# Normed tiles of the second pass turned through memory and VectorE instead of TensorE, with loads moved to GpSimd's queue

## The chip, the cores and the metric

The kernel runs on one core of a Trainium2 chip. The metric is device time in microseconds: the median of the runs shown, each the time of one execution. TensorE is written PE, VectorE DVE, ScalarE ACT, GpSimd POOL, and SP is the engine that here only issues DMAs.

## What is computed

Two layers on `x` of 8 x 32 x 32 x 512, all in float32:

```python
# layer 0: group norm, 8 heads of 64 over 1024 tokens, out projection, residual
xn  = group_norm(x) * gn_scale + gn_bias
q, k, v = split(xn @ w_qkv + b_qkv)
x   = x + (softmax(q @ k.T / 8 per head) @ v) @ w_out + b_out          # "mid"

# layer 1: attention on 256 sampled tokens, then a norm and an MLP
h   = layernorm(x) * ln_g + ln_b                                       # "hat"
o   = gelu(depthwise_conv7x7(h @ wq + bq, stride 2) + dw_b)
pos = grid + tanh(o @ pw_w)                                            # 256 places per image
s   = bilinear_sample(x, pos)                                          # "smp"
q   = (h @ wq + bq) @ mq_w + mq_b;  k = (s @ wv + bv) @ mk_w + mk_b;  v likewise
z   = softmax(q @ k.T per head) @ v @ mo_w + mo_b + x
out = gelu((layernorm(z) * ln_g + ln_b) @ mlp_w + mlp_b) + z
```

## The kernel before

The kernel makes two passes over the images. The first (layer 0) writes two things to memory: the residual `mid` and the normed, turned features `hat_d`. It also does most of the convolutions. The second pass, which the change concerns, goes over 16 half images `hi`, and over 4 head pairs `hp` in each: 64 units, numbered `n`. A unit computes scores for 512 queries of two heads, their softmax, its turn, and the product with the values.

The order of work inside a pass is written out by hand. `at(place, step)` puts a step at a place on a line whose whole numbers are units, and `run_due` issues all steps sorted by place. Each engine then executes its instructions in that order, each waiting for what it reads and for a free buffer. Inside a plain unit the steps are:

- `scores` at n: PE makes `sc`, DVE the negated maxima `nmax`, ACT the exponentials `e`.
- `moved` at n + 0.02 and n + 0.04, `taken` at n + 0.0401 and n + 0.041: DVE turns 32x32 blocks of `e` into `sq`; SP writes `sq_d` and reads it back as `et`, so that the keys lie on the partitions. `share` and `spread` send the reciprocal sums the same way (`rs_d`, `inv`).
- `query_step` at n + 0.042: PE's product of `hat_h` and the folded weight `wA`, for the next unit's queries.
- `product` at n + 1.1 and `scale` at n + 1.2: PE's `av` of the unit before, and DVE's `attH`.

Beside them, `back_steps` finishes one tile of 128 tokens per unit, four tiles per half image:

- `fetch` and `add`: a residual tile `xr` from `mid`, to which POOL adds a bias row. They come in pairs of tiles.
- `joined`: PE multiplies `attH` with `wo`, DVE adds `xr` to give `z`, and takes its statistics (`stats`, `mv`); POOL raises the variance to the power -0.5.
- `norm`: DVE makes the normed tile `zn`.
- `turned`: PE transposes `zn` in four pieces of 128x128, and ACT copies the result as `zT` from PSUM.
- `mlp`, `biased`, `gelu`, `end`: the product of `zT` with `wm` (its rows scaled by `ln_g`), a bias row, gelu on ACT for two tiles at a time, then POOL adds `z` and stores the tile.

Three more strands are laid between. `conv_steps` makes the convolutions of the last two images, in chunks of 49 taps on two lanes: DVE alone (`chunk<-pad,dww,chunk`, five taps a unit, three in some), and ACT with POOL (`parts`, then `chunk<-parts,chunk`); each chunk begins with two products `mm<-wq_r,hat`. These taps run in about the first 36 units. `point_steps`, once per image, turns a finished convolution into places (`offsets`, `targets`), gathers the rows (`gather`) and weighs them on DVE (`sample`); `key_step` and `value_step` then multiply `smp`. `fetch_hat` loads a half image of `hat_d`, 1 MB, in one DMA.

The buffers that matter: three PSUM tiles `mm` that all of these products share, two buffers each for `et`, `zn`, `zT` and `hat_h`, and four for `xr`.

In the profile nearly all instructions carry line 54, since the helper `InOrder` records every operation there; they are told apart by their tiles. Matmuls in float32 appear as two records each.

Of the kernel before, what the change touches and what calls it, by code (L numbers as in the profile page):

```python
# [17 lines left out]
P = 128  # L18
# [3 lines left out]
C = 512  # L22
# [225 lines left out]
def attention_then_deformable_attention(  # L248
# [126 lines left out]
    def at(place, step):  # L375
        due.append((place, len(due), step))
# [654 lines left out]
    with ExitStack() as l1:  # L1031
# [15 lines left out]
        def load_small():  # L1047
            with nc.allow_non_contiguous_dma(reason="small vectors onto partitions"):
                for t, v in ((lng, ln_g), (lnb, ln_b)):
                    nc.sync.dma_start(t, v.rearrange("(c p) -> p c", p=P))  # L1050

        def load_conv():
            nc.sync.dma_start(dww, dw_w.rearrange("(c p) a u v -> p c (a u v)", p=P))
# [32 lines left out]
        def conv_load(b):  # L1086
            room[b, "o"] = cv.tile([P, NC, NS], F32, tag="o", name="o")
            nc.sync.dma_start(room[b, "o"], o_d[b][:, :, :])
# [27 lines left out]
        def offsets_turned(b):  # L1116
            room["th"] = turn_offsets(room["tanh"])
# [29 lines left out]
        def fetch_hat(hi):  # L1147
            hat[hi] = raw.tile([P, NC, C], F32, tag="hat", name="hat_h", bufs=2)
            nc.sync.dma_start(hat[hi], hat_d[hi // 2][:, ts(hi % 2, NC), :])

# [23 lines left out]
        def tmp(name, bufs):  # L1177
            return work.tile([P, C], F32, tag=name, name=name, bufs=bufs)

        def back_steps(hi, start, step, tail=False):  # L1180

            b, half = divmod(hi, 2)
            xs = mid[b].rearrange("(t p e) c -> e t p c", e=2, p=P)[half]
            outs = out_tok[b].rearrange("(t p e) c -> e t p c", e=2, p=P)[half]
            xr, z, zn, zT, res = {}, {}, {}, {}, {}
            n_units = 2 * B * NHP

            def fetch(t):
                xr[t] = tmp("xr", 4)
                nc.sync.dma_start(xr[t], xs[t])  # L1190

            def add(t):
                nc.gpsimd.tensor_tensor(xr[t], xr[t], bo_row, ALU.add)

            def joined(t):
                ps = project(lambda c: attH[hi][:, c, ts(t, P)], lambda c: wo[:, c, :])
                z[t] = tmp("z", 4)
                nc.vector.tensor_tensor(z[t], ps, xr[t], ALU.add)
                stats = work.tile([P, 6], F32, tag="stats", name="stats")
                mv = xr["mv", t] = work.tile([P, 3], F32, tag="mv", name="mv")  # L1200
                nc.vector.bn_stats(stats, z[t])
                nc.vector.bn_aggr(mv[:, 0:2], stats)
                rstd(mv[:, 2:3], mv[:, 1:2], 1e-5)

            def norm(t):
                zn[t], mv = tmp("zn", 2), xr["mv", t]
                nc.vector.tensor_scalar(
                    zn[t], z[t], mv[:, 0:1], mv[:, 2:3], ALU.subtract, ALU.mult
                )

            def turned(t):
                ps = mm_tile()
                for c in range(NC):
                    nc.tensor.transpose(ps[:, ts(c, P)], zn[t][:, ts(c, P)], ident)
                zT[t] = tmp("zT", 2)
                for half in range(2):
                    nc.scalar.copy(zT[t][:, ts(half, C // 2)], ps[:, ts(half, C // 2)])

            def mlp(t):
                res["ps", t] = project(lambda c: zT[t][:, ts(c, P)], lambda c: wm[:, c, :])  # L1220

            def biased(t):
                res[t] = tmp("res", 3)
                nc.vector.tensor_tensor(res[t], res["ps", t], bm_row, ALU.add)

            def gelu(t):
                nc.scalar.activation(res[t], res[t], AF.Gelu)

            def end(t):
                (nc.vector if tail else nc.gpsimd).tensor_tensor(res[t], res[t], z[t], ALU.add)  # L1230
                (nc.sync if tail else nc.gpsimd).dma_start(outs[t], res[t])

            for t in range(NC):
                over, eve = (start + step * t >= n_units - i and not tail for i in range(2))
                n, pair = start + step * t, start + step * (t - t % 2)

                ends = (n + 0.6, n + 1.03, n + 1.0392)
                if eve:
                    ends = (n + 0.61, n + 0.72, n + 0.73) if over else (n + 1.06, n + 1.62, n + 1.625)
                places = (pair - 1.6, pair - 0.5), (n + 0.012, n + 0.03), ends  # L1240
                if tail:
                    turn = n + 0.15 + 0.005 * (t > 0)
                    places = (n - 0.7, n - 0.6), (n, n + 0.01), (turn, n + 0.25, n + 0.26)
                steps = (fetch, add), (joined, norm), (turned, mlp, biased)
                for place, what in zip(sum(places, ()), sum(steps, ())):
                    at(place, lambda t=t, what=what: what(t))


                ends = [t - 1, t] if t % 2 and not tail else [t] if tail else []

                for what, after in (
                    (gelu, 0.27 if tail else 0.735 if over else 1.72),
                    (end, 0.28 if tail else 0.74 if over else 2.24),
                ):
                    for i in ends:
                        at(n + after, lambda i=i, what=what: what(i))
# [33 lines left out]
        def conv_steps():  # L1290
            for lane, chunks in enumerate(((0, 3, 6), (1, 2, 4, 5, 7))):
                free = 0.5 + lane
                for k in chunks:
                    b, cb = EARLY + k // NC, k % NC
                    first = next(n for n in range(60) if n + 0.49 > free)
                    fills = [first + 0.49, first + 0.55]
                    at(fills[0] - 1.8, lambda b=b, cb=cb: conv_fetch(b, cb))
                    for par, place in enumerate(fills):
                        at(place, lambda b=b, cb=cb, par=par: fill(b, cb, par))
                        at(place + 0.02, lambda lane=lane, par=par: fill_end(lane, par))  # L1300
                    unit = int(fills[1]) + 1
                    i = 0
                    while i < KS * KS:
                        points = unit % (2 * NHP) in (NHP - 1, NHP, NHP + 2)
                        count = 7 if lane else 3 if points else 5
                        for j in range(count):
                            if i == KS * KS:
                                break
                            place = 0.25 + 0.01 * j if not lane else 0.045 + 0.001 * j if j < 4 else 0.65 + 0.01 * j
                            at(unit + place, lambda b=b, cb=cb, i=i, lane=lane: tap(b, cb, i, lane))  # L1310
                            free = unit + place
                            i += 1
                        unit += 1

        def point_steps(b):
            last = 2 * NHP * b - NHP
            at(last - 3.5, lambda: conv_load(b))
            at(last - 2.035, lambda: conv_gelu(b))
            at(last - 1.465, lambda: offsets(b))
            at(last - 1.36, lambda: offsets_turned(b))  # L1320
            at(last - 0.959, lambda: targets(b))
            for h, (p0, p1) in enumerate(((-0.28, 0.0415), (1.72, 2.0415))):
                at(last + p0, lambda h=h: gather(b, h))
                at(last + p1, lambda h=h: sample(b, h))
            first = 2 * NHP * b
            for hp, place in enumerate((-0.82, -0.815, 0.185, 1.18)):
                at(first + place, lambda hp=hp: key_step(b, hp))
            for t, place in enumerate((-0.81, 0.18)):
                at(first + place, lambda t=t: value_step(b, t))

        def load_late():
            nonlocal bq_row, wo, wm, bo_row, bm_row, wq_r
            wo = load_w(late2, mo_w, "wo")
            wm = load_w(late2, mlp_w, "wm")
            bo_row = load_row(late, mo_b, "bo_row")
            bm_row = load_row(late2, mlp_b, "bm_row")
            bq_row = load_row(wp, bq, "bq_row")
            load_conv()
            wq_r = load_w(first, wq, "wq_r")
# [21 lines left out]
            point_steps(b)  # L1361
        for hi in range(2 * B):
            if hi > 1:
                at(NHP * (hi - 1) - 1, lambda hi=hi: fetch_hat(hi))
            if hi + 1 < 2 * B:
                back_steps(hi, NHP * (hi + 1) + 1, 1)
            else:
                back_steps(hi, NHP * (hi + 1) + 0.65, 0.1, tail=True)
# [34 lines left out]
```

## Time and profile before

| | |
|---|---|
| median of 3 runs | 3359.01 us (3353.66 to 3364.82) |
| profiled execution | 3361.59 us, of which the span 3359.9 us |
| mean granted TensorE clock | 0.991 |
| the second pass begins | about 2155 us into the span |
| busy time in the span | PE 3274.0, DVE 2496.4, ACT 1810.1, POOL 1545.1 us |
| moved by DMA | 643.61 MB, mean 192 GB/s |

All numbers in the steps below come from this one profiled execution. Busy time of PE is an upper view, because matmuls are pipelined and their ends are modelled. Where an engine waited for several things, the profile names the one that came last. Where a group's mean is larger than busy time divided by count, its instructions overlapped.

### The profile page before, as it was taken

Reading aid. Unit: us, or ns where it says so; the run is one execution under the profiler, and the core shown is the slowest. Engines: PE = TensorE matmul, PEld = TensorE weight load, DVE = VectorE, ACT = ScalarE, POOL = GpSimd, SP = SyncE. Lnnn points to the kernel's source line nnn. Section 1 sums busy time; section 2 is a strip of 40 time slices with the busy share of each in tenths; the row PEclk is TensorE's granted clock in tenths of the full one; section 3 lists DMA queues with packets and bytes.
Section 4 is the critical chain, followed back from the end, with each engine's and each line's share of the span. In section 5 each row is a group of like instructions: output and inputs, shape, how many; then the busy total and the mean of one; then the engine's idle time right before and its main releaser. Section 6 shows DMA issues by size and latency. Waiting matters only on the chain.

```text
span 3359.9 us, 59630 instructions
## 1 busy us (share of the span) xinstructions
PE 3274.0 (97%) x21736; PEld 1335.3 (40%) x21736; DVE 2496.4 (74%) x3381; ACT 1810.1 (54%) x3927; POOL 1545.1 (46%) x1905
## 2 busy tenths in 40 slices
PE   7999999999999999999999999889999999999998
PEld 3344444344444344344444443333333333333333
DVE  5777778888888898888888886348677686665654
ACT  3443356576576566566566564135566555654442
POOL 1001226746746755765665663205555454642222
PEclk9999999999999999999999999899999999999999
DMA  5666766776776767776766667356666565665753
GB/s 151 178 181 163 208 180 184 226 182 183 213 194 174 220 193 187 203 203 176 216 195 172 199 193 218 117 195 220 193 206 200 191 203 185 214 219 191 228 178 131
DMA packets 442180, 643.61 MB, mean 192 GB/s; under 512 B 73152, under 2 KB 236992, under 8 KB 439840
## 3 DMA queue, kind: packets, MB, share of 16 engines
q1 hardware_dynamic: 409232, 531.93, 55.0%
q0 software_dynamic: 30928, 104.73, 10.0%
q8 instruction: 172, 2.82, 0.3%
q10 hardware_dynamic: 1728, 3.15, 0.2%
q14 instruction: 120, 0.98, 0.1%
HBM read 247.43 MB, written 123.73 MB: 110 GB/s over the span
## 4 chain that ended last, share of the span: by engine, by line
PE 88%; DVE 3%; ACT 3%; POOL 2%; issue 2%; DMA 1%; SPq 0%; ACTq 0%; POOLq 0%; DVEq 0%
PE mm L54 55%; PE sc L54 17%; PE av L54 16%; ACT e L54 2%; POOL chunk L54 1%; DVE nmax L54 1%; DVE sq L54 1%; DMA et<-sq 1%; SPq L54 0%; POOL res L54 0%; POOL xr L54 0%; DMA row<-mid,ii 0%; DVE smp L54 0%; DVE stats L54 0%; ACT parts L54 0%
## 5 line engine op out<-in xcount | busy, mean ns | idle before, releaser
L54 ACT ACTIVATE e<-sc,nmax 128x1024 f32<-128x1024 f32 (+1 forms) x1024 | 803.1, 797 | 487.7 <-DVE nmax L54 486.3
L54 DVE TENSOR_REDUCE nmax<-sc 128x1 f32<-128x1024 f32 (+1 forms) x640 | 751.6, 1215 | 343.4 <-PE sc L54 343.0
L54 POOL TENSOR_TENSOR oa<-part_x,oa 128x256 f32<-128x256 f32 x852 | 638.6, 750 | 551.8 <-ACT part_x L54 505.6
L54 DVE STREAM_TRANSPOSE sq<-e 128x1024 f32<-128x1024 f32 x640 | 766.1, 1228 | 158.1 <-ACT e L54 137.8
L54 ACT ACTIVATE part_x<-pad_x,dww_x 128x256 f32<-128x256 f32 x852 | 441.6, 545 | 253.1 <-POOL oa L54 251.5
L54 PE MATMUL sc<-k,q 64*64 64x512 f32 x4096 | 516.2, 604 | 10.2 <-ACT e L54 7.2
L54 PE MATMUL av<-et,v 128*64 128x256 f32 x4096 | 501.2, 387 | 9.2 <-DMA et<-sq 5.5
L54 PEld LDWEIGHTS av<-et,v 128*64 128x64 f32 x4096 | 273.8, 137 | 325.9 <-issue 158.0
L54 POOL TENSOR_TENSOR mv<-mv,minus_half 128x1 f32<-128x1 f32 x128 | 76.5, 598 | 500.7 <-DVE mv L54 500.3
L54 POOL TENSOR_TENSOR chunk<-parts,chunk 128x256 f32<-128x256 f32 x240 | 188.2, 784 | 256.8 <-ACT parts L54 242.7
L54 PEld LDWEIGHTS sc<-k,q 64*64 64x64 f32 x4096 | 139.5, 132 | 317.7 <-issue 206.4
L54 PE MATMUL mm<-w,attT 128*64 128x512 f32 x1024 | 233.8, 600 | 11.7 <-DVE attT L54 11.7
L54 PE MATMUL mm<-xT,wB 128*64 128x512 f32 x1024 | 233.0, 597 | 3.2 <-issue 3.2
L54 DVE SCALAR_TENSOR_TENSOR od<-pad_x,dww_x,od 128x256 f32<-128x256 f32 x276 | 231.1, 837 | 5.5
L54 PE MATMUL mm<-wo,attH 128*64 128x512 f32 x1024 | 234.7, 600 | 0.0
L54 PE MATMUL mm<-wC,xT 128*64 128x256 f32 x2048 | 232.1, 379 | 0.0
L54 PE MATMUL mm<-wm,zT 128*64 128x512 f32 x1024 | 230.7, 592 | 1.0 <-ACT zT L54 1.0
L54 PE MATMUL mm<-hat_h,wA 128*64 128x512 f32 x1024 | 230.9, 593 | 0.0
L54 PE MATMUL mm<-xT,wA 128*64 128x512 f32 x1024 | 230.7, 592 | 0.0
L54 ACT ACTIVATION_READ_ACCUMULATOR e<-sc,nmax 128x1 f32 x1024 | 209.4, 204 | 0.0
L54 ACT ACTIVATE parts<-pad,dww 128x256 f32<-128x256 f32 x240 | 126.4, 552 | 126.9 <-POOL chunk L54 125.9
L54 PEld LDWEIGHTS mm<-wC,xT 128*64 128x64 f32 x2048 | 147.6, 137 | 78.1 <-issue 6.4
(182 smaller groups left out, 3503.7 us busy)
## 6 DMA issues: line engine op xcount, KB each, us to landing
et<-sq SPq DMA_DIRECT2D x2048, 128.0 KB, 2.9
sq_d<-sq SPq DMA_DIRECT2D x128, 512.0 KB, 2.7
et<-sq_d SPq DMA_DIRECT2D x128, 512.0 KB, 4.4
inv<-rs_d SPq DMA_DIRECT2D x256, 128.0 KB, 4.7
hat_h<-hat_d SPq DMA_DIRECT2D x16, 1024.0 KB, 8.3
xr<-mid SPq DMA_DIRECT2D x64, 256.0 KB, 5.7
xr<-in_x_dram POOLq DMA_DIRECT2D x62, 256.0 KB, 3.9
x<-in_x_dram POOLq DMA_DIRECT2D x60, 256.0 KB, 4.3
```

The costliest lines, as they stand in the source:

```text
L54: return self.tc.keep_in_program_order(op(*args, **kwargs))
```

## The change

In 58 of the 64 tiles of the second pass, PE no longer transposes `zn`. Instead the normed tile is written to memory (`away`), read back with its tokens and channels regrouped so that every 32x32 block already lies in the right place (`back`), and the blocks are turned by one DVE instruction (`blocks`), which gives `zT` directly. The four tiles of the tail and the last two before them keep the transposes (`by_matmul`). The channel order on the partitions differs between the two layouts, so the rows of `wm`, `ln_g` and `ln_b` are loaded in the new order, with four DMAs each, and the six remaining tiles write `zn` with its channels regrouped.

The residual rows are fetched by POOL's queue instead of SP's, and earlier (2.6 units ahead of the pair instead of 1.6; the add 1.45 instead of 0.5). From the third half image on, `hat_h` comes in four quarters by POOL's queue, one per unit.

Places change too: `mlp` follows the product for the next queries instead of preceding it, `biased` follows later in the unit, `end` comes at the beginning of a unit, the steps of `point_steps` come about a unit earlier, and the units with a sample have two DVE taps instead of three.

```diff
@@ load_small: the same for ln_g and ln_b
-                    nc.sync.dma_start(t, v.rearrange("(c p) -> p c", p=P))
+                    for r in range(NSQ):
+                        nc.sync.dma_start(
+                            t[ts(r, SQ)], v.rearrange("(r c i) -> r i c", r=NSQ, c=NC)[r]
+                        )
@@ beside fetch_hat, which still loads the first two half images
+        def fetch_part(hi, c):
+            if c == 0:
+                hat[hi] = raw.tile([P, NC, C], F32, tag="hat", name="hat_h", bufs=2)
+            nc.gpsimd.dma_start(hat[hi][:, c, :], hat_d[hi // 2][:, hi % 2 * NC + c, :])
@@ back_steps
             def fetch(t):
                 xr[t] = tmp("xr", 4)
-                nc.sync.dma_start(xr[t], xs[t])
+                nc.gpsimd.dma_start(xr[t], xs[t])
...
             def norm(t):
                 zn[t], mv = tmp("zn", 2), xr["mv", t]
+                to, src = zn[t], z[t]
+                if by_matmul(t):
+                    to = to.rearrange("p (c r i) -> p r c i", r=NSQ, c=NC)
+                    src = src.rearrange("p (r c i) -> p r c i", r=NSQ, c=NC)
                 nc.vector.tensor_scalar(
-                    zn[t], z[t], mv[:, 0:1], mv[:, 2:3], ALU.subtract, ALU.mult
+                    to, src, mv[:, 0:1], mv[:, 2:3], ALU.subtract, ALU.mult
+                )
+
+            def by_matmul(t):
+                return tail or start + step * t >= n_units - 1
+
+            def away(t):
+                zn["d", t] = dram.tile([NSQ, P, P], F32, tag="zn_d", name="zn_d", bufs=3)
+                nc.sync.dma_start(
+                    zn["d", t].rearrange("r p x -> p r x"), zn[t].rearrange("p (r x) -> p r x", r=NSQ)
+                )
+
+            def back(t):
+                zn["l", t] = tmp("zn", 2)
+                nc.sync.dma_start(
+                    zn["l", t], zn["d", t].rearrange("r (q k) x -> (r q) (k x)", k=NSQ)
+                )
+
+            def blocks(t):
+                zT[t] = tmp("zT", 2)
+                nc.vector.transpose(
+                    zT[t].rearrange("p (c q k) -> p k c q", c=NC, q=SQ),
+                    zn["l", t].rearrange("p (k c i) -> p k c i", k=NSQ, i=SQ),
                 )
...
-                ends = (n + 0.6, n + 1.03, n + 1.0392)
+                ends = (n + 0.0301, n + 0.0405, n + 1.013, n + 1.05, n + 1.15)
...
-                places = (pair - 1.6, pair - 0.5), (n + 0.012, n + 0.03), ends
+                places = (pair - 2.6, pair - 1.45), (n + 0.012, n + 0.03), ends
...
-                steps = (fetch, add), (joined, norm), (turned, mlp, biased)
+                turns = (turned,) if by_matmul(t) else (away, back, blocks)
+                steps = (fetch, add), (joined, norm), (*turns, mlp, biased)
...
-                    (end, 0.28 if tail else 0.74 if over else 2.24),
+                    (end, 0.28 if tail else 0.74 if over else 2.0125),
@@ conv_steps
-                        points = unit % (2 * NHP) in (NHP - 1, NHP, NHP + 2)
-                        count = 7 if lane else 3 if points else 5
+                        points = unit % (2 * NHP) in (NHP - 1, NHP + 1)
+                        count = 7 if lane else 2 if points else 5
@@ point_steps
-            at(last - 3.5, lambda: conv_load(b))
-            at(last - 2.035, lambda: conv_gelu(b))
-            at(last - 1.465, lambda: offsets(b))
-            at(last - 1.36, lambda: offsets_turned(b))
-            at(last - 0.959, lambda: targets(b))
-            for h, (p0, p1) in enumerate(((-0.28, 0.0415), (1.72, 2.0415))):
+            at(last - 4.5, lambda: conv_load(b))
+            at(last - 3.035, lambda: conv_gelu(b))
+            at(last - 2.465, lambda: offsets(b))
+            at(last - 2.36, lambda: offsets_turned(b))
+            at(last - 1.959, lambda: targets(b))
+            for h, (p0, p1) in enumerate(((-1.4, -0.959), (0.0125, 1.041))):
                 at(last + p0, lambda h=h: gather(b, h))
                 at(last + p1, lambda h=h: sample(b, h))
@@ load_late
-            wm = load_w(late2, mlp_w, "wm")
+            wm = late2.tile([P, NC, C], F32, tag="wm", name="wm")
+            for r in range(NSQ):
+                nc.sync.dma_start(
+                    wm[ts(r, SQ)], mlp_w.rearrange("(r c i) o -> r i c o", r=NSQ, c=NC)[r]
+                )
@@ the loop over half images
             if hi > 1:
-                at(NHP * (hi - 1) - 1, lambda hi=hi: fetch_hat(hi))
+                for c in range(NC):
+                    place = NHP * (hi - 1) - 1 + (c + 0.65 if c < NC - 1 else NC - 0.7)
+                    at(place, lambda hi=hi, c=c: fetch_part(hi, c))
```

## The prediction

> **What bounds the kernel now.** I read the page first, for the engines over the whole span.
>
> ```profile
> PE 3274.0 (97%) x21736; PEld 1335.3 (40%) x21736; DVE 2496.4 (74%) x3381; ACT 1810.1 (54%) x3927; POOL 1545.1 (46%) x1905
> ...
> PE   7999999999999999999999999889999999999998
> ```
>
> PE is busy in nearly every slice. Since a busy PE may still be slow, the second view is the table by stretches, for the second pass (columns: stretch, length, busy time of PE, PEld, DVE, ACT and POOL with instruction counts, granted clock, DMA share, GB/s). The first row lies in the part of the pass that also runs the convolution taps, the second behind it.
>
> ```profile
> 2400.00:2600.00 200.00, 198.67 (x1220) 74.77 (x1216) 146.80 (x255) 118.02 (x318) 109.68 (x129) 1.00 0.62 203
> 3000.00:3200.00 200.00, 200.00 (x1266) 77.28 (x1264) 124.94 (x194) 90.02 (x267) 57.59 (x62) 1.00 0.65 211
> ```
>
> The clock is full, and DVE, the next engine, has 27% left with the taps and 38% without. Third, PE in order of time for one plain unit (start, us, engine, operation).
>
> ```profile
> 3015.61 1.96 PE L54 MATMUL sc<-keys,q 64*64 64x256 f32 x32
> 3017.50 3.65 PE L54 MATMUL mm<-wo,attH 128*64 128x512 f32 x16
> 3020.98 3.60 PE L54 MATMUL mm<-wm,zT 128*64 128x512 f32 x16
> 3024.42 3.60 PE L54 MATMUL mm<-hat_h,wA 128*64 128x512 f32 x16
> 3027.85 1.89 PE L54 MATMUL av<-et,vals 128*64 128x512 f32 x8
> 3029.67 0.66 PE L54 MATMUL mm<-ident,zn 128*128 128x128 f32 x4
> 3030.25 1.96 PE L54 MATMUL sc<-keys,q 64*64 64x256 f32 x32
> ```
>
> There is no gap. A plain unit lasts 14.64 us, and from the start of the four transposes to the next scores 0.58 us pass: that is what a tile's transposes cost. The three units before it last 14.64 or 14.65 too, so PE's own work sets the pace. Last, whom PE waited for from 2160 us on.
>
> ```profile
> PE mm L54 <- DVE smp L54: 13.3, 2, 9.0
> PE mm L54 <- DVE zn L54: 5.1, 5, 1.3
> PE mm L54 <- DVE res L54: 4.7, 3, 1.6
> PE sc L54 <- ACT q L54: 4.4, 2, 4.0
> ```
>
> The 13.3 us are the two gathers that open the pass, which stay. What can be won beyond the transposes is about 10 us.
>
> **The change, part by part.** Rows for the costs, from the groups of 2150 to 3360 us and from the DMA issues (last number: us from issue to landing):
>
> ```profile
> L54 PE MATMUL mm<-ident,zn 128*128 128x128 f32 x256 | 41.9, 286 | 5.1 <-DVE zn L54 5.1
> L54 ACT COPY zT<-mm 128x256 f32<-128x256 f32 x128 | 41.1, 372 | 76.5 <-PE mm L54 75.1
> L54 DVE STREAM_TRANSPOSE sq<-e 128x1024 f32<-128x1024 f32 x128 | 158.5, 1238 | 54.2 <-ACT e L54 54.2
> L54 POOL DMA_DIRECT2D out_dram<-res x60 | 35.2, 587 | 21.9 <-POOL res L54 17.2 <-issue 4.6
> ```
>
> ```profile
> sq_d<-sq SPq DMA_DIRECT2D x128, 512.0 KB, 2.7
> et<-sq_d SPq DMA_DIRECT2D x128, 512.0 KB, 4.4
> ...
> xr<-mid SPq DMA_DIRECT2D x64, 256.0 KB, 5.7
> ```
>
> *Removed from PE.* Of 64 tiles, 4 in the tail and the 2 at n = 63 and 64 keep the transposes; 58 lose them: 58 x 0.58 = 33.6 us, all on PE's path. (Busy time gives 58 x 41.9/64 = 38.0; I take the spacing.) The 5.1 us in which PE waited for zn go too, as PE no longer reads it in these tiles. The Trainium skill ("VectorE: DVE Perf Modes", section on the three transpose paths) gives 390 ns for one 128x128 bf16 transpose on TensorE, which would make 58 x 4 x 0.39 = 90 us; no row here shows that price. It also says that VectorE turns blocks of 32x32 only, which is why a trip through memory has to move the blocks.
>
> *Removed from ACT.* 116 copies of 372 ns, 43 us. ACT waits for others here: 0 on the path.
>
> *Added to DVE.* 58 block transposes of 128x512. Half of the 128x1024 row (1238 ns) is 0.62 us; the writes go out four elements apart, which no row shows, so the upper end is 1.24 (half speed), the lower 0.5 (the spacing of the simplest 128x512 operation, zn). I take 0.62, since the taps that read at stride two show no loss for it (339 ns for 256 elements, against 615 for zn's 512). It stands between the statistics and the first sq transpose, where DVE waited 54.2 us in all for e. That cover hides it in units without lag; without cover it costs what is worked out below.
>
> *Added to SP's queue.* 58 writes and 58 reads of 256 KB. The write waits for zn; behind it wait rs_d and the second sq_d, both fed by later DVE work, so it delays nothing. The read waits for the write, and for its place behind the first et load, which itself waits for the end of av. Behind it stand the second et load and inv. So the read is issued at about 14.7 us of a plain unit, the write having landed long before (sq_d, twice as large: 2.7 us). Landing: 4.4 us (et) at best, 5.7 (xr of the same size, issued later in the same burst) taken. The new deadline: wm follows wo and wA now, so starts 1.89 + 3.49 + 3.43 = 8.8 us into the next unit of 14.06 us; less 0.6 for the block transpose, the data must be there 14.06 + 8.8 - 0.6 - 14.7 = 7.5 us after issue. It fits by 1.8 us. The second et load comes about 1 us later and is needed only at 26 us, where about 20 is expected: 0.
>
> *Moved to POOL's queue.* 64 residual rows and 56 quarters of hat: 120 x 0.587 = 70 us over 1140 us, on an engine that stood 344 us waiting for mv and 243 us for parts. They are issued one unit ahead or more and no longer stand in SP's burst: 0 on PE. The bound is an indirect issue (982 ns), 118 us in all, still inside these waits. DVE pays, if at all, through contention, and the trace has it (DVE in order of time):
>
> ```profile
> 2531.39 2.56 DVE L54 SCALAR_TENSOR_TENSOR chunk<-pad,dww,chunk 128x256 f32<-128x256 f32 x5
> ...
> 2605.98 5.55 DVE L54 SCALAR_TENSOR_TENSOR chunk<-pad,dww,chunk 128x256 f32<-128x256 f32 x3
> ```
>
> 0.51 us a tap while POOL stood still, 1.85 while it added xr and res. The adds stay, and mostly shift within the unit. An issue's cost to the taps: between 0 and its own length, 0.59 us; I take 0, since the issue writes no tile. The rule against the move is in the Trainium skill, "SBUF — State Buffer", section on the wrong bandwidth-pool intuition: a DMA from GpSimd's queue took 3100 ns instead of 620 when a DVE copy held the shared port. By that figure 120 issues would cost POOL 300 us more and the gain would shrink to the second rival's; the 587 ns above were measured beside a busy DVE and do not show it.
>
> *The new wait: wm for zT.* Without lag DVE runs: nmax ends 4.2 us after the scores began, z waits for wo until 5.4, z and statistics take 1.74 (2613.71 to 2615.45 in that unit), the block transpose 0.6, so zT stands at 7.8, before 8.8. If DVE is free only D us into a unit, zT comes at D + 2.3 + 1.7 + 0.7 = D + 4.7, and PE stalls D - 4.1. In a tap unit DVE ends with attH at 14.55 (av's end) and five taps (0.51 to 1.1 each, mean 0.77): 18.4, so D = 4.3, stall 0.2. With a sample (4.0 to 5.0) and two taps: about 19, D = 5, stall 0.9. This bites where PE has no extra product: 13 units of the tap part (11 to 13, 19 to 22, 27 to 30, 35, 36). 13 x 0.5 = 7 us taken; 0 to 20 as bounds, with slow taps and a slow block transpose. The same places lost time before, through zn and res.
>
> *The point steps a unit earlier, two taps instead of three.* The samples end a unit sooner than the keys need them: of the 4.7 us for res I take back 2 (0 to 4.7). The 4.0 us wait for q comes in the short units 3 to 5 that have no wm; a sample takes the place of the targets there: +1 (0 to +2).
>
> *Opening and tail.* Nine more DMA issues of some 0.4 us on SP, ahead of loads that PE needs 20 us later, while PE waits for gathers: 0 (to +3.6). Tail: four residual rows by POOL, where the add waited 4.7 us for them: 0 (-2 to +3).
>
> Sum: -33.6 - 5.1 - 2 + 7 + 1 = -32.7 us. The profiled execution took 3361.6 us (span 3359.9 and 1.7 around it), so 3328.9; it lay 2.6 us above the median of 3359.0, so **3326 us** as a median.
>
> **Rivals.** *DVE lag eats half* (0.2): taps near 1.1 us or a 1.24 us block transpose make each of the 13 units stall 2 us: 26 instead of 7, so 3326 + 19 = 3345. For it: 1.85 us taps occur, and the tolerance of PE falls, since zT now hangs on this unit's DVE. Against it: the xr adds, which made z wait 10.6 us, come a unit earlier.
>
> *The read lands late: slower* (0.1). One mechanism: the read sits between the two et loads on SP, and past 7.5 us from issue every plain unit stalls by the excess. There are 30 of them (the 13, units 37 and 38, and 15 later ones). It decides against the change past 7.5 + 32.7/30 = 8.6 us. At 9.5 us: 3326 + 60 = 3386. For it: the hat loads of the convolution, 512 KB in 512-byte pieces, take 8.6 us, and DMA share must rise from 0.65. The addition: 0.52 MB on 211 x 14.64 = 3.09 MB, so 257 GB/s. Against it: single microseconds behind the scores ran at 300 to 348 GB/s.
>
> *More than the sum* (0.1): the rest of the waits for res (2.7) and that for q (4.0 and the 1 added) vanish, and no new ones (7) come: 3326 - 14.7 = 3311.
>
> *It does not do what it says:* the written-out order has 58 writes, 58 reads, 120 moved loads and six tiles with transposes left, so only PE's "busy" could deceive; the gapless 14.64 us units speak against that.
>
> **How the numbers follow.** Forecast 0.6, lag 0.2, late read 0.1, more 0.1. The range, 3309 to 3348, reaches to the case of more and to the lag rival with a few us of scatter between runs, and leaves out the late read and the worst lag. Faster by over 0.3% (10 us, about what a measurement of this kernel can tell from no change): 0.6 + 0.1 + most of the lag case, 0.82; same 0.06; slower 0.12.
>
> **What would show it.** Right: plain units of 14.06 us in the table behind the taps, mm<-ident,zn at x24, PE's wait for DVE zT below 10 us, the read landing in 5 to 6 us, DVE busy up by 36 us. Wrong: waits of mm for zT above 30 us; if DVE then waits for the DMA zn<-zn_d it was the late read, if not the lag; or POOL issues far above 0.6 us.

## The result, and the profile after

| | before | after |
|---|---|---|
| median of the runs taken together | 3361.6 us | 3393.4 us (3379.4 to 3394.8) |
| ratio, 95% interval | | 1.0079 (1.0059 to 1.0099) |
| profiled execution, span | 3359.9 us | 3386.7 us |
| first scores of the second pass at | 2216.6 us | 2225.7 us |
| from there to the last unit's scores | 1078.2 us | 1094.2 us |

The kernel became slower by 32 us by the medians (27 by the ratio), where 33 us less had been forecast; the time lies outside the range. The last two rows use the start of the first `sc` matmul of a unit in the timeline of PE. They divide the 26.8 us of the spans into 3.1 in the first pass (the same instructions; it ends here with the last wait of `mm` for `attT`), 6.0 at the opening of the second, 16.0 in the units and 1.7 in the tail.

The page first (engines, and PE's slices), then the table by stretches for the two stretches that were shown of before, with the same columns.

```profile
PE 3254.8 (96%) x21504; PEld 1322.3 (39%) x21504; DVE 2546.2 (75%) x3439; ACT 1791.1 (53%) x3823; POOL 1607.8 (47%) x2025
...
PE   7999999999999999999999999789999989999998
```

```profile
2400.00:2600.00 200.00, 191.41 (x1174) 71.32 (x1174) 152.40 (x234) 107.80 (x288) 114.32 (x141) 0.99 0.73 231
3000.00:3200.00 200.00, 187.04 (x1162) 70.56 (x1162) 127.78 (x206) 83.38 (x242) 67.84 (x84) 0.99 0.79 244
```

The transposes are gone from 58 tiles (the group of those that are left, from 2150 us on):

```profile
L54 PE MATMUL mm<-ident,zn 128*128 128x128 f32 x24 | 3.9, 285 | 0.3 <-DVE zn L54 0.3
```

PE's busy time fell by 19 us only, of 38 in the transposes, partly since other matmuls became slower (last section). And PE, which was busy for all 200 us of the second stretch before, now stands still for 13 of them. No other engine is near its limit. So the loss is made of waits and of what follows them. PE in order of time shows where:

```profile
3128.28 1.96 PE L54 MATMUL sc<-keys,q 64*64 64x256 f32 x32
...
3140.49 3.65 PE L54 MATMUL mm<-wm,zT 128*64 128x512 f32 x16 [3.23 <-DVE zT L54]
...
3145.79 1.96 PE L54 MATMUL sc<-keys,q 64*64 64x256 f32 x32
...
3159.84 1.53 PE L54 MATMUL sc<-keys,q 64*64 64x256 f32 x24
```

The second of these two units lasts 14.05 us, 0.59 less than a plain unit before, as the sum had it. The first lasts 17.51: PE waits 3.23 us for `zT`. Behind the taps such a wait comes in six units (43, 45, 47, 51, 53 and 55). Over the second pass (whom PE waited for: us, times, longest):

```profile
PE mm L54 <- DVE zT L54: 42.3, 21, 3.8
PE mm L54 <- DVE smp L54: 17.8, 2, 11.1
PE av L54 <- DMA et<-sq_d: 5.3, 3, 3.2
PE mm L54 <- DMA hat_h<-hat_d: 3.5, 2, 3.2
```

Of the 42.3 us, 24.6 fall before 2920 us (taps) and 17.7 behind. Behind, but for one of 3.1 in the last unit, VectorE itself was waiting, for the read. The next lines follow the late one above. SP issued the read at 3128.84, when POOL had just issued two stores, a quarter of `hat_h` and two residual rows; four gathers followed from 3129.10 on. VectorE got the data at 3139.26.

```profile
3128.84 1.58 SPq L54 DMA_DIRECT2D zn<-zn_d  x1
```

```profile
3126.58 0.54 POOL L54 DMA_DIRECT2D hat_h<-hat_d  x1
3127.11 1.07 POOL L54 DMA_DIRECT2D xr<-mid  x2
```

```profile
3139.26 1.09 DVE L54 STREAM_TRANSPOSE zT<-zn 128x512 f32<-128x512 f32 x1 [3.49 <-DMA zn<-zn_d]
```

```profile
3128.00:3134.00 6.00, 6.00 (x52) 2.47 (x52) 4.39 (x14) 2.39 (x11) 4.08 (x5) 1.00 1.01 311
3134.00:3140.00 6.00, 3.26 (x16) 0.86 (x12) 2.41 (x5) 3.96 (x9) 3.59 (x4) 1.00 1.07 357
```

From issue to use 10.4 us passed, against a deadline of 7.5. In the two stretches of 6 us the DMA engines are full (share 1.01 and 1.07), although the mean over 3000 to 3200 is 0.79. Who had them: queue by queue (q0 is POOL's, q1 SP's; packets, MB, share of the engines' time) in the 6.76 us from the read's issue on, and in the same stretch of the same unit of a_sp, which has the rows and `hat_h` back on SP's queue:

```profile
q0 software_dynamic: 383, 1.24, 52.6%
q1 hardware_dynamic: 637, 0.97, 48.2%
```

```profile
q1 hardware_dynamic: 1172, 1.55, 73.6%
q0 software_dynamic: 178, 0.54, 21.1%
```

With the loads on it, POOL's queue had half of the engines, and SP's queue moved 0.97 MB where it moves 1.55. The median does not show this; the groups of DMA issues say 4.9 us for the read:

```profile
xr<-mid POOLq DMA_DIRECT2D x64, 256.0 KB, 6.3
zn<-zn_d SPq DMA_DIRECT2D x58, 256.0 KB, 4.9
```

### The profile page after: what moved, and what is told of

Its sections match the earlier page's. It is cut to its first block, busy times and chain, and to the rows that moved or that the text cites. A ratio compares the mean times of both kernels' runs of the same rounds, so it can differ in the third digit from the quotient of the medians.

```text
span 3386.7 us, 59407 instructions
## 1 busy us (share of the span) xinstructions
PE 3254.8 (96%) x21504; PEld 1322.3 (39%) x21504; DVE 2546.2 (75%) x3439; ACT 1791.1 (53%) x3823; POOL 1607.8 (47%) x2025
## 4 chain that ended last, share of the span: by engine, by line
PE 82%; DMA 5%; DVE 4%; POOL 4%; issue 2%; ACT 2%; SPq 1%; ACTq 0%; POOLq 0%; DVEq 0%
PE mm L54 51%; PE sc L54 16%; PE av L54 16%; DMA zn<-zn_d 2%; POOL chunk L54 1%; ACT e L54 1%; SPq L54 1%; DMA et<-sq 1%; DVE nmax L54 1%; DVE sq L54 1%; POOL xr L54 1%; DMA hat_h<-hat_d 1%; POOL row L54 1%; POOL res L54 0%; DMA zn_d<-zn 0%
## 5 line engine op out<-in xcount | busy, mean ns | idle before, releaser
L54 PE MATMUL mm<-wm,zT 128*64 128x512 f32 x1024 | 238.3, 608 | 43.4 <-DVE zT L54 42.3
```

Of the source, the lines that this page charges most:

```text
L54: return self.tc.keep_in_program_order(op(*args, **kwargs))
```

## The experiments

All comparisons are with runs of before on the same chip. "Units 0-43" and "43-63" are lengths in the profiled execution, from scores to scores: the part with taps (its last few units have none) and the part behind. Each is from one execution: h_small and after, whose units are the same, differ by 1.6 and 2.1 us, so a difference of about 2 us there shows nothing.

| kernel | ratio to before (95%) | units 0-43 | units 43-63 |
|---|---|---|---|
| before | 1 | 755.1 | 323.1 |
| after | 1.0079 (1.0059 to 1.0099) | 764.8 | 329.5 |
| a_sp: loads back to SP | 0.9984 (0.9973 to 0.9996) | 748.6 | 316.7 |
| a_xr: rows back | 1.0030 (1.0020 to 1.0040) | 761.5 | 319.4 |
| a_hat: quarters back | 1.0021 (1.0009 to 1.0032) | 752.8 | 322.4 |
| q_act: loads by ACT | 1.0036 (1.0021 to 1.0051) | 750.6 | 326.8 |
| b_pool: before, loads by POOL | 1.0079 (1.0064 to 1.0094) | 779.3 | 323.1 |
| a_busy: a_sp, POOL kept as busy | 0.9993 (0.9982 to 1.0004) | 750.8 | 316.4 |
| c_dense: after, dense transpose | 1.0085 (1.0071 to 1.0099) | 759.4 | 333.0 |
| a_dense: a_sp, dense transpose | 0.9971 (0.9960 to 0.9983) | 746.8 | 314.9 |
| a_fewtap: a_sp, 20 taps less | 0.9974 (0.9962 to 0.9986) | 740.8 | 317.9 |
| f_wm: after, wm behind av | 1.0114 (1.0096 to 1.0132) | 764.8 | 347.8 |
| d_split: before, split loads | 1.0022 (1.0013 to 1.0031) | 755.2 | 323.1 |
| h_small: after, loads later | 1.0074 (1.0053 to 1.0094) | 763.2 | 331.6 |
| a_fh: a_sp, f_wm, h_small | 0.9979 (0.9968 to 0.9990) | 745.8 | 320.6 |
| a_open: a_sp, other opening | 0.9968 (0.9956 to 0.9981) | 747.0 | 315.9 |
| a_blk: a_open, transpose earlier | 0.9985 (0.9975 to 0.9995) | 745.1 | 327.2 |

**The moved loads alone: a_sp and b_pool.**

```diff
@@ a_sp: after with
-                nc.gpsimd.dma_start(xr[t], xs[t])
+                nc.sync.dma_start(xr[t], xs[t])
...
+                at(NHP * (hi - 1) - 1, lambda hi=hi: fetch_hat(hi))    # instead of the four fetch_part
@@ b_pool: before with the opposite edit, and the rows' places (pair - 2.6, pair - 1.45)
```

> The kernel after, with the residual rows and hat_h (whole, at its old place) back on SP's queue; everything else stays. Theory 1 (the read of zn is late because the transfers of POOL's queue run beside it and the et loads, instead of standing in line): reads of 10 us disappear, the largest landing falls from 11.6 to about 6 us; PE's wait for zT behind the taps (2920 us on) falls from 17.7 to below 5 us; the time falls by 10 to 18 us against the kernel after (3393), to about 3378. Rival (only the added volume counts, whichever queue moves it): the wait stays at 15 to 20 us and the time within 5 us of the kernel after.

> The kernel before, with only the moves to POOL's queue (residual rows 2.6 units ahead, hat_h in quarters). Theory 1: alone they cost little, since before has no read of zn with a short deadline: at most 5 us of new waits for et, time within 5 us of before (3361.6). Rival (POOL's 120 issues hold up VectorE's taps and POOL's own adds): DVE busy rises by 10 us or more, PE's waits for zn and res rise above the 9.8 us of before, time 10 us or more above before.

Median 3356.8 us for a_sp: the two loads that the sum had moved at no cost are worth 36.6 us by the medians (32 by the ratios), twice what the theory expected, and with them back the change beats before by a little. In the units it is 29.0 us, 16.2 with taps and 12.8 behind. a_sp also undoes the cutting of `hat_h` into quarters and their places; no run has quarters on SP's queue. For b_pool the theory was wrong and the rival right in time: 3389.7 us, 24.2 us more in units 0 to 43 and nothing behind. VectorE's busy time rose by 14 us, as the rival had it, but the waits that it named, for `zn` and `res`, did not rise. Instead PE waited 9.1 us for `attH` and, four times, 8.5 us in all for quarters of `hat_h`, neither of which stands among the waits of `mm` in before. The waits of a_sp (PE, then DVE):

```profile
PE mm L54 <- DVE zT L54: 25.6, 19, 3.5
```

```profile
DVE zT L54 <- DMA zn<-zn_d: 4.3, 5, 1.7
```

VectorE's wait for the read was 18.3 us (9 times) in after; now it is 4.3. The same bytes move, so volume alone does not make the read late. What PE still waits behind the taps (3.4 us) falls in units 43, 45, 51 and 53, in which POOL's queue carries gathers.

**Which load, and which queue: a_xr, a_hat, q_act.** The first undoes only the first line of the diff above, the second only the quarters; q_act puts `nc.scalar` where after has `nc.gpsimd` for both.

> The kernel after, with only the residual rows back on SP's queue (hat_h still in quarters by POOL's). It splits the 36 us that both moves cost together. By bytes and issues: rows are 64 of 120 issues and 16 of 31 MB, so an even split gives about 3375. If the late read comes from the rows, which are issued in pairs just as the et loads start: behind the taps (43 to 63) the units fall by 10 us or more of the 13 that both gave back. If it comes from the quarters: less than 4. In the tap part, ACT's wait of parts for POOL falls by about half of the 15.5 us that both gave.

> The kernel after, with only the quarters of hat_h back (whole, by SP's queue, at the old place), the rows stay on POOL's. Complement of a_xr. If the two moves add: a_xr took 13.3 us off the units, both 29.0, so this takes 15.7, nearly all before unit 43 (764.8 to 751), and the late reads behind the taps stay (329.5 to 326 or more); time near 3376.

> The kernel after, with the residual rows and the quarters of hat_h issued by ACT's queue at the same places, instead of POOL's. If any second queue beside SP's makes the read of zn late: units 43 to 63 stay near after's 329.5 and far above the 316 that they take with SP's queue. If it is POOL's queue as such: they fall to 316 to 319. In the tap part ACT's issues stand in front of the exponentials, so there the time can rise or fall: 750 to 775.

Behind the taps a_xr gives 10.1 of the 12.8 us back, as expected: the rows, issued in pairs in every second unit, make most of the late reads. But a_hat gives 7.1 there, where less than 4 was expected: either load moved back takes half or more, as full engines would have it. Among the taps the quarters cost most (12.0 us go when they go back, 3.3 for the rows). With ACT's queue 10.2 of the 12.8 us behind the taps remain, so it is not POOL's queue as such; this is the line of DVE in q_act from 2970 us on (16.4 us, 7 times, in after):

```profile
DVE zT L54 <- DMA zn<-zn_d: 10.7, 5, 3.5
```

The late step is another one there, though. The read was issued 2.0 to 6.9 us into the unit in the five units that waited (0.6 where nothing delays it), because the write ahead of it had taken 6.1 to 11.0 us to land; the read itself then took at most 7.4. What a second queue delays is the whole trip of `zn`, now the one half and now the other. Among the taps, however, q_act is nearly as good as a_sp. That part of the loss belongs to POOL's queue.

**Is it POOL's time? a_busy.**

```diff
+        def stand_in():
+            nc.gpsimd.tensor_tensor(idle, idle, minus_half[:, 0:1], ALU.pow)
@@ a_sp, with stand_in() at each place where after has POOL issue a row or a quarter
```

> The kernel a_sp (after, with the moved loads back on SP's queue), plus 120 tiny POOL operations on an own 128x1 tile (power, 0.56 us each as the trace has it for mv) at the places where POOL issued the rows and quarters. It puts back POOL's time without the transfers. If POOL's time made the loss in the taps (POOL delays the sums of the ACT lane, ACT waits with its next tap in front of the exponentials): units 0 to 43 lengthen by about 16 us over a_sp's 748.6, ACT's wait of parts for POOL grows by some 15 us, units 43 to 63 stay at 316.7, time near 3372. Rival (the loss in the taps is the transfers' too): units 0 to 43 within 4 us of a_sp, time the same as a_sp.

ACT's wait between taps, before 2920 us, in a_sp and in a_busy (after had 130.9):

```profile
ACT parts L54 <- POOL chunk L54: 115.4, 132, 6.3
```

```profile
ACT parts L54 <- POOL chunk L54: 134.4, 133, 5.7
```

The wait grew by 19 us as expected, the units by only 2.3 (3.8 against a_open, which has the same taps). The wait is real and costs little, hardly more than the scatter: the theory that POOL's time made the loss falls. The traces divide the 16.2 us among the taps. PE's waits are 10.3 us longer in after than in a_sp (for `zT` 24.6 against 19.1, for quarters of `hat_h` 3.5 against 0, the rest small), and matmuls behind long waits are slower by 5.9 (last section).

The quarters came late because POOL issued them late. The last one of a half image has its place 0.74 units ahead of its use. In unit 31 of after POOL issued it 3.8 us before PE was ready for it, and it took 6.9 us to land. In b_pool, in the three units with waits of 2.2 to 3.8 us, it was issued 0.1 to 2.6 us before PE was ready. With ACT's queue it was at least 7.9 us, and PE did not wait. That is one reason why ACT's queue avoids this part. The growth of the waits for `zT` lies in the third unit behind a sample: 3.1, 3.2, 2.3 and 3.2 us in units 14, 22, 30 and 38, against 1.2 at most in a_sp. In a_busy three of these four are 2.3 to 2.5, so POOL's time may have a share in it; the rest is open.

**The block transpose's price: c_dense, a_dense.**

```diff
-                    zT[t].rearrange("p (c q k) -> p k c q", c=NC, q=SQ),
+                    zT[t].rearrange("p (c k q) -> p k c q", c=NC, q=SQ),
```

> The kernel after, with the block transpose writing its 32-element rows dense instead of four elements apart; the rows of these 58 product tiles then stand in another order (tokens permuted inside a tile), the work is the same. Theory 2 (the spread write makes the transpose slow, and this feeds the stall of VectorE's lag): the transpose takes about 0.62 us instead of 1.12, DVE busy falls by 29 us from 2546, PE's wait for zT in the tap part falls from 24.7 to about 12 us, behind the taps by less than 4; time 10 to 15 us below the kernel after. Rival (lag comes from the taps and the order, the transpose is hidden): zT wait falls by less than 6, time within 5 us of the kernel after. If the transpose stays at 1.1 us, the spread write is not its cause.

> The kernel a_sp with the dense block transpose (0.62 us hoped for in the sum on record; rows inside a tile permuted, so that the output stands in another order). If the stalls left in a_sp (zT, 22.5 us without the tail) are VectorE's lag of D + 4.7 us, with 0.5 us of it the spread write: 14 stalls shorter by up to 0.5 each, units 0 to 43 shorter by 5 to 7 us, time near 3351. Rival (the lag is made ahead of DVE, by late exponentials or the read): less than 2 us.

The group of block transposes (count, busy, mean ns) in after, and in c_dense:

```profile
L54 DVE STREAM_TRANSPOSE zT<-zn 128x512 f32<-128x512 f32 x58 | 64.8, 1117 | 18.3 <-DMA zn<-zn_d 18.3
```

```profile
L54 DVE STREAM_TRANSPOSE zT<-zn 128x512 f32<-128x512 f32 x58 | 40.8, 703 | 23.1 <-DMA zn<-zn_d 23.1
```

Writing four elements apart costs 0.41 us per transpose, 24 us of VectorE in all. It brought nothing in time on after (1.0085 against 1.0079), and 3.5 us in the units of a_sp, of which 1.8 are among the taps, within the scatter: it is hidden or nearly so. The rivals were right.

**Lag behind the samples: a_fewtap, a_blk.**

```diff
@@ a_fewtap: a_sp with
+                            if lane or not points:
                                 at(unit + place, lambda b=b, cb=cb, i=i, lane=lane: tap(b, cb, i, lane))
@@ a_blk: a_open with
-                ends = (n + 0.0301, n + 0.0405, n + 1.013, n + 1.05, n + 1.15)
+                ends = (n + 0.0301, n + 0.0405, n + 1.011, n + 1.05, n + 1.15)
```

> The kernel a_sp with the two VectorE taps of each unit with a sample left out (20 taps, which are missing from the convolution sums). If samples and taps in one unit make the lag in units 12 to 14, 20 to 22, 28 to 30, 36 to 38: about 1.9 us less lag behind each sample; the stalls of 0.9, 1.2 and 1.6 us go, units 0 to 43 shorter by 8 to 12 us, time near 3347. Rival: less than 3 us.

> The kernel a_open with the block transpose one place earlier in VectorE's queue: ahead of z and the statistics (n + 1.011) instead of behind them. It then starts 1.7 us earlier after a late unit; with VectorE free D us into the unit zT comes at D + 3.4 instead of D + 5.1, and D is about 4.6 behind a sample. If the stalls are this place: the 14 waits of 0.9 to 1.6 us in the taps go, units 0 to 43 shorter by 12 to 16 us than a_open's 747.0, time near 3339. Rival (VectorE lacks the time, so z and then sq are late instead): PE waits for attH or et instead, less than 4 us gained. In units without lag the transpose now waits for the read and holds z: up to 1 us there, hidden if zT's product has slack.

Without the 20 taps units 0 to 43 took 7.7 us less, just short of what was expected. But 2.1 of that lie ahead of unit 12, and 2.9 in unit 29, where a_sp had a late read. The waits of 0.9 and 1.2 us went; the one of 1.6 became 2.3, which in two units cost 1.9 more in slow matmuls. So samples and taps in one unit make the lag in the first and third unit behind a sample; why the second grew is open. The transpose ahead of `z` (a_blk) gained 2 us among the taps, no more than the scatter, and lost 11 behind them, because now VectorE waits for the read with all its other work behind it (second pass):

```profile
DVE zT L54 <- DMA zn<-zn_d: 46.8, 19, 7.5
```

That is the rival, in a form that had been put at "up to 1 us".

**Slack for zT: f_wm.**

```diff
-                ends = (n + 0.0301, n + 0.0405, n + 1.013, n + 1.05, n + 1.15)
+                ends = (n + 0.0301, n + 0.0405, n + 1.013, n + 1.11, n + 1.21)
```

> The kernel after, with wm behind av (mlp at n + 1.11, its bias at n + 1.21); the moved loads stay on POOL's queue. Theory (zT comes up to 3.8 us late, for whatever cause, and PE has no other product to put there): each of the 21 waits shrinks by av's 1.72 us, 42.3 to about 13 us, time near 3364. Rival (the lateness is an engine's or the DMA rings' lack of capacity, not of slack): the wait moves to av for et or to later units, the sum of PE's waits falls by less than 10 us and the time stays above 3383.

```profile
PE av L54 <- DMA et<-sq_d: 41.7, 19, 4.4
```

The wait moved whole, 42.3 us for `zT` in after and 41.7 for `et` now. The kernel became slower (1.0114): PE's waits in units 43 to 63 are 4.7 us longer than in after and its matmuls 13.6 us slower (last section). `et` shares the burst with the read and is as late; a place for one is taken from the other.

**The opening: d_split, h_small, a_open, and all together: a_fh.**

```diff
@@ d_split: before, with lng, lnb and wm in four DMAs of 32 partitions
-                    nc.sync.dma_start(t, v.rearrange("(c p) -> p c", p=P))
+                    for r in range(NSQ):
+                        nc.sync.dma_start(t[ts(r, SQ)], v.rearrange("(c p) -> p c", p=P)[ts(r, SQ)])
@@ prep in h_small: fetch_hat(1) first; load_small and the repeated vectors around load_late, behind the samples
@@ a_open: the same order, and lng, lnb, wo, wm, bo_row, bm_row by nc.gpsimd, behind the gathers
```

> The kernel before, with only ln_g, ln_b and wm loaded in four DMAs of 32 partitions each, in the old channel order. Theory 3 (nine more DMAs at the opening delay lnb and the second hat_h, and through VectorE's queue the samples): first scores of the second pass 5 to 7 us later than before's 2216.6, time 4 to 8 us above before. Rival (the opening's 6 us come from another part, such as POOL's loads): first scores within 2 us of before, time the same.

> The kernel after, with the eight small loads and the two repeated vectors behind the second hat_h and the samples at the opening. Theory 3 (the split loads stood in the way of the samples, as the split alone cost 6.2 us in the kernel before): PE's wait for smp falls from 17.8 to about 13, first scores about 6 us earlier than after's 2225.7, time about 3387. Rival (the wait for the memory they write lies ahead of load_late now and delays wo and wm): first scores earlier, but as much lost in the first two units, time the same.

> The kernel a_sp with an opening in another order: second hat_h at once, the small loads, wo, wm and the bias rows by POOL's queue behind the gathers, the two repeated vectors behind the samples. The gathers then have no transfer beside them. If the split loads (6 us) and the loads beside the gathers made PE wait for the samples: smp wait from 19.9 to below 13, first scores some 7 us earlier, time near 3350. Rival (wo, wm come too late now, rows and units 0 to 2 pay it back): time the same as a_sp.

> All three remedies: loads back on SP's queue, wm behind av, small loads behind the samples. If the causes add: 3356.8 for the queue, less 22 (19 waits for zT of 25.6 us, each shorter by 1.72), less 6 for the opening: about 3329, close to the 3326 that the sum on record gave for the change alone. If wm behind av only moves the wait to et: about 3345.

d_split costs 6.2 us by the medians and nothing in the units: this is the opening's 6.0. From the last wait of the first pass for `attT` to the first scores it takes 73.7 us (before 67.3, after 73.4). SP's issues of `ln_g` in d_split (start, us from the first to the last of the four), and its waits there for stores of `hat` (us, times, longest):

```profile
2160.15 25.21 SPq L54 DMA_DIRECT2D lng<-in_L_conv_ln_g_dram  x4
```

```profile
SPq L54 <- DMA hat_d<-hat: 19.6, 4, 16.4
```

In the order of instructions every transfer of SP and ACT waits for the one eight places earlier, whose completion counter it uses: the traces show eight such counters, taken in turn. In before the longest wait there for a store of `hat` was 7.2 us. Four loads in place of one reach the counter of a later store, and wait 16.4 us for it. Everything behind them on SP, `lnb` and the second `hat_h`, and through VectorE the samples, came late. h_small won 2.8 us of it (70.6); in it, as in after, `wo` and `wm` ran beside the second gather. a_open puts these behind the gathers in one queue: 67.5 us (a_sp 74.2), and a time of 3352.8 us, the best version run, 0.32% below before. a_fh stood at 3354.9, not near 3329: its middle part brings nothing (units 0 to 63 in 1066.4 us, a_sp 1065.2), as f_wm had shown.

## Why the prediction was wrong, by its own steps

*Removed from PE: right.* Plain units without a stall last 14.05 us instead of 14.64, which is 0.59 us for each of 58 tiles, and the waits for `zn` are gone.

*Moved to POOL's queue, "0 on PE": the step that failed.* The sum looked at POOL, which had the time: 547 and 568 ns an issue in after, no longer than the 587 taken, and the 3100 ns of the rule weighed there did not show. VectorE's taps did not pay for the issues either: in units 0 to 43 of after the 55 taps that overlapped one and no other work of POOL took 0.49 us, the 29 that overlapped nothing 0.48. The cost lay in the DMA engines. On SP's queue the rows and `hat_h` stood in line with `et`; on another they run beside `et`, `zn_d` and the read, in the same few us: 29.0 us in the units (a_sp). A smaller part is that "one unit ahead or more" did not hold for the last quarter of a half image, whose place is 0.74 units ahead and which POOL issued later still: 3.5 us of waits in after, 8.5 in b_pool.

*The read, 5.7 us against a deadline of 7.5.* The median, 4.9, is even better. But the deadline holds for each tile, and the six late ones behind the taps took 7.3 to 11.0 us. Two of them (units 45 and 53) were also issued 1.4 and 2.9 us late, since the write, which the sum had as long landed (2.7 us), took 6.0 and some 7.5. The rival "the read lands late" had the right sign and deadline, but it did not see the cause, which stood in another step at 0. Its size (3386) came out by luck: it put 2 us on 30 units, and behind the taps six units waited 14.6 us in all. Its evidence against, 300 to 348 GB/s in single microseconds, is no room to spare: with full engines the burst ran at 311 and 357. (The convolution's loads, 8.6 us there, have a median of 8.8.)

*The new wait, 7 us, bounds 0 to 20.* It was 42.3. With the loads back it is 22.5 without the tail, mostly in waits of 0.9, 1.6 and 1.2 us in the three units behind a sample. Eight of the sum's thirteen units waited, 11.5 us in all; the other half fell in units that it had not named, 14, 37 and 38 among them. So VectorE's lag was right as a mechanism, and the mean of 0.5 us per unit and the list of units were too small. The price of the transpose, 1.12 instead of 0.62 us and just inside its bound of 1.24, is 3.5 us of that at most.

*The opening, 0 to +3.6.* It was 6.2 (d_split). The sum counted issues; the cost was a wait that came with their number.

*Together.* In the profiled executions the forecast was -32.7 and the result +26.8 us: 29.0 for the loads, 6.0 for the opening, 19.7 for the other waits of the units and the slower matmuls behind them, a term that the sum did not have (a_sp's units are 13.0 us shorter than before, where -32.7 was forecast), and 4.7 in the first pass and the tail, where nothing explains more than scatter between executions.

The Trainium skill ("DMA: Bandwidth & Descriptors", section on queues, rings and completion order) says that a DMA engine "round-robins between the queue rows it has work for". The runs fit this: POOL's queue had 52.6% and SP's 48.2% of the engines' time in the stretch above, and units 43 to 63 took 329.5 and 326.8 us with the loads on a second queue, 316.7 without. It speaks against moving loads away from the queue in which a transfer with a deadline stands.

## What to carry to other kernels

A load that moves to an idle engine's queue is not free because that engine is: it leaves the line it stood in and runs beside the transfers that were ahead of it. So price it at the transfer with the nearest deadline, in the busiest few microseconds, not by the mean DMA share and not by the median landing. And count transfers, not only bytes and issue times: each one more can wait for an older one that it has nothing to do with.

## What the runs showed of the hardware

After a wait of 2 us or more PE often ran slowly. In the second pass of the seventeen kernels the sixteen 512-wide matmul records of an `mm` took 3.65 or 3.66 us after each of 196 waits below 2.0 us; after 79 longer ones they took more in 42 cases, 5.0 to 6.6 us, the shortest such wait being 2.09 us. Two short waits can do it together: in a_fh one of 0.76 and one of 1.57 us with two matmul records between them were followed by a clock of 0.50. The table by stretches of after, around a wait of 3.13 us that ended at 2460.43, shows the granted clock at 0.50:

```profile
2460.40:2463.00 2.60, 2.56 (x6) 0.85 (x8) 1.67 (x2) 2.60 (x13) 2.28 (x3) 0.50 0.16 61
```

So a stall of 3 us can cost 1.4 to 3 us more than it lasts. Over units 0 to 43 the mean granted clock was 0.996 in before, 0.993 in a_sp and 0.984 in after. The Trainium skill ("TensorE: Matmul & The Clock Gate", Part 1) puts the fall to the half clock after an idle window of about 3.4 us; here waits from 2.09 us on were enough, at times.
